# Two transformer layers on one core: feed forward's root on VectorE, layer 1's shifts by one product for two query blocks, new ranks and paces

## The chip, the cores and the metric

One core of a Trainium2 chip runs the whole program. Five engines work at the same time, each through its own queue: TensorE (PE; its weight loads are listed as PEld), VectorE (DVE), ScalarE (ACT), GpSimd (POOL) and SyncE (SP), which here only starts transfers. The metric is the device time of one execution in microseconds (us); less is better.

## The reference

Input x is 4 sequences (B) of 512 positions (T) by 128 channels (D), float32. There are 16 heads of 8 channels in both layers.

```python
xn = layernorm(x)                                   # layer 0
s = attention0(xn, ...)                             # below
g = silu(moe0(xn))
x = x + s * g
xn = layernorm(x)                                   # layer 1
s = block1(xn, ...)                                 # below
g = silu(moe1(xn))
x = x + s * g

# attention0: q, k with RMS norm per head, 4 value heads; mask: j <= i and j >= i - 64
a = (q @ k.T / sqrt(8)) * mask
denom = mean(sigmoid(a), axis=-1) + 0.5             # over all 512 keys
fitness = 1 / (denom * sum(1 / denom, over queries))
s = softmax(a * fitness[:, None] - 1e10 * (1 - mask)) @ v @ w_o + b_o

# moe0: 8 experts 128 -> 512 -> 128, GELU; a token goes to the larger index of its top two; times 2

# block1: layernorm, then windows of 64 positions that start 16 before every multiple of 32 ...
attn = softmax(q[window] @ k[window].T / sqrt(8)); wo = attn @ v[window]
# ... each window's first part is blended linearly with the one before; then
h = out @ wproj + bproj + xn
s = gelu(layernorm(h) @ w1 + b1) @ w2 + b2 + h      # feed forward, 128 -> 512 -> 128

# moe1: 8 experts 128 -> 512 -> 128, ReLU; a token goes to the expert of the largest logit
```

Layer 1's input is normed twice: once before the layer, once inside `block1`, whose residual is the first norm's result.

## The kernel before

All of x stays on the chip. The work is cut into threads, Python generators such as `scores_k1` or `feed1`. Most of them run over batches b = 0 to 3, and within one over four tiles of 128 positions, 16 tiles in all; the expert threads run over 23 blocks of up to 128 tokens of one expert.

**Order.** Which thread goes next is decided when the program is built, not by hand. `run` holds for every thread what its next step needs, takes the thread whose needs are there first in a modelled time, and among equal ones the one with the lowest rank for its batch (the four numbers behind each thread, L1485 on). `spent(cost, steps, events)` moves the modelled time on by `pace()` times TensorE's cost and places the step's work on VectorE ("D"), ScalarE ("A") and GpSimd ("G") in modelled queues; `copied` uses them to choose ScalarE or VectorE for a copy. TensorE works in the order in which the threads issue. On the other engines the order is fixed as the program is built, after the threads' order and the instructions' dependences. Where the model has a gap on TensorE, `awake` puts in products of `ones16` whose result is overwritten (warm-up products).

**Layer 0.** `prepare0` norms x and transposes it (`tr_xn`, `xnT`), `logits` gives the gate's `lg`, `route` works out which token goes into which block (`off`, `tok_blk`, `in_place`, and the product `tokens`). `moe_x` gathers blocks (`xb`, an indirect transfer by GpSimd, and its transpose `xt`), `moe_h` and `moe_y` do the two expert products (h, y) and put results back (`yt`, indirect too). `project0`, `scores_q` (s tiles, maxima `mx`, tanh `th`, sums `sm`), `fitness0`, `scores_k` (e tiles, exponentials `pt`), `values0` (`ov`), `outs0` and `combine0` are the attention.

**Layer 1.** `prepare1` norms (`xr`, `xn1`, transposed as `tr_xn1`) and gives the gate's logits; `project1` norms a second time and makes keys and queries `kd`, `qd`. `queries1` does a tile of 128 positions: the masked keys `k4` on VectorE, masked queries `q4` on GpSimd, values `v`, the s tile (scores with queries as rows, 32 products), and the maxima over keys `mx` (L1290). The maxima, negated, are the softmax's shift. The second score tile e, with keys as rows, needs that shift along its columns. So `split` (L465) writes each as three bf16 terms into `shb`, which is transposed (`tr_sh`), copied by ScalarE (`shd`, L1298) and multiplied by four masks (`sh4`, L1301; the trace calls it `sh`). `scores_k1` adds it: e is 32 products of kd and q4 and, on top, products of a matrix of ones with `sh4`:

```python
for w in range(2):
    for g in range(G):
        r = slice(32 * g, 32 * g + NS * J)
        mm(
            ps[g // 2][w * KB : (w + 1) * KB, g % 2, par], ones16[r, 0:KB],
            sh4[r, par, :, w * KB : (w + 1) * KB], start=False, stop=True,
        )
```

`w` is one of two query blocks of 64 (KB) in a tile, `par` one of the two overlapping sets of windows, `g` a group of four heads. `values1`, `outs1`, `contexts1` finish the attention. `feed1` (twice a batch, for two tiles each) does the product `pr`, the norm's moments `mv_d`, the root `rs_d`, `hn`, its transpose `tr_hn`, the two products f and fy. `combine1` writes the result. The experts run beside it, as in layer 0.

**The two roots.** `rsqrt` is an addition on VectorE (L392) and a power of -1/2 on GpSimd (L393). `rsqrt_many` (L395) does the root on VectorE by shifts and three Newton steps, 13 operations; layer 0's RMS norm uses it. `feed1` calls `rsqrt` (L1434).

Of the kernel before, what the change touches and what calls it, by code (L numbers as in the profile page):

```python
# [57 lines left out]
def two_layers(  # L58
# [22 lines left out]
    def mm(*args, **kw):  # L81

        ins = nc.tensor.matmul(*args, **kw)  # L83
        tc.stamp_issue_order_token(ins.ins, "pe")
        return ins
# [185 lines left out]
    def after(event):  # L271

        return None, max(0.0, at[event] - max(now["T"], now["-"]))
# [53 lines left out]
    def pace():  # L327
        return 1.8 if now["T"] < 70.0 else 1.12
# [66 lines left out]
    def rsqrt_many(dst, src, scale, eps):  # L395

        n = dst.shape[1]
        x = small.tile([P, n], F32, tag="rq_x", name=f"rq_x_{dst.tensor.name}", bufs=1)
        nc.vector.tensor_scalar(x, src, scale, eps, ALU.mult, ALU.add)
        y = small.tile([P, n], F32, tag="rq_y", name=f"rq_y_{dst.tensor.name}", bufs=1)  # L400
        nc.vector.tensor_single_scalar(y.bitcast(I32), x.bitcast(I32), 1, ALU.logical_shift_right)
        nc.vector.tensor_scalar(y.bitcast(I32), y.bitcast(I32), -1.0, float(0x5F3759DF), ALU.mult, ALU.add)
        nc.vector.tensor_scalar_mul(x, x, -0.5)
        z = small.tile([P, n], F32, tag="rq_z", name=f"rq_z_{dst.tensor.name}", bufs=1)
        for i in range(3):
            nc.vector.tensor_tensor(z, y, y, ALU.mult)
            nc.vector.tensor_tensor(z, z, x, ALU.mult)
            nc.vector.scalar_tensor_tensor(dst if i == 2 else y, z, 1.5, y, ALU.add, ALU.mult)
# [83 lines left out]
    def route(mask, n):  # L492
# [7 lines left out]
        with tc.high_priority():  # L500
# [53 lines left out]
            spent(0.35, [("D", 1.0)] * 7, [("rows", n)])  # L554
            in_places = []
            for q in range(2):
# [5 lines left out]
                spent(0, [after(("rows", n)), ("D", 1.2)], [("places", n, q)])  # L562
# [351 lines left out]
    shbs1 = prepared("shb1_", 2, [P, 2, G, 32], BF16)  # L914
    later.close()
# [288 lines left out]
    def project1():  # L1204

        for b in range(B):
            yield "-", [("xn1", b), ("s1", (b - 1) * NT - 1)]
# [30 lines left out]
    def queries1():  # L1238


        for i in range(NTILE):
# [52 lines left out]
            split(shb, mx, f"1_{b}_{t}")  # L1294
            spent(1.15, [("D", 2.45), ("D", 1.0)], [("s1", i), ("shb", i)], scores=1)
            yield "M", [("shb", i), ("e1", i - 2)]
            shd = att_p.tile([P, 2 * P], BF16, tag="shd1", name=f"shd1_{b}_{t}")
            nc.scalar.copy(shd, transposed16(shb.rearrange("p a g r -> p a (g r)"), 2, f"sh1_{b}_{t}"))  # L1298
            sh4 = att_p.tile([P, 2, J, P], BF16, tag="sh4_1", name=f"sh4_1_{b}_{t}")
            for j in range(J):  # L1300
                nc.vector.tensor_scalar_mul(sh4[:, :, j], shd.rearrange("p (a f) -> p a f", a=2), smask[:, j : j + 1])  # L1301
            asked1[i] = q4, sh4, v
            spent(0.13, [("A", 0.4), ("D", 1.2)], [("sh1", i)])

    def scores_k1():
        for i in range(NTILE):
# [9 lines left out]
            for par in range(2):  # L1316
# [8 lines left out]
                for w in range(2):  # L1325
                    for g in range(G):
                        r = slice(32 * g, 32 * g + NS * J)
                        mm(
                            ps[g // 2][w * KB : (w + 1) * KB, g % 2, par], ones16[r, 0:KB],
                            sh4[r, par, :, w * KB : (w + 1) * KB], start=False, stop=True,  # L1330
                        )
# [3 lines left out]
            spent(1.45, [("Ae", 1.03), ("Ae", 1.03)], [("e1", i)], scores=2)  # L1335
# [77 lines left out]
    def feed1():  # L1413


        for b in range(B):
            for u in range(0, NT, 2):
# [53 lines left out]
    def combine1():  # L1471
# [13 lines left out]
        (moe_h(0, gelu), 0, 59, 111, 16),  # L1485
        (scores_k1(), 87, 25, 32, 64),
        (project1(), 92, 81, 14, 102),
        (queries1(), 107, 26, 4, 78),
        (combine0(), 19, 20, 21, 22),
        (moe_load(0, xd0, w1_0, C_B1_0), 109, 42, 85, 68),  # L1490
        (moe_load_2(0, w2_0, b2_0), 18, 74, 23, 2),
        (gates(0, yt0), 56, 5, 6, 8),
        (values1(), 66, 112, 86, 55),
        (prepare0(), 31, 65, 95, 50),
        (moe_load(1, xd1, w1_1, C_B1_1), 35, 84, 34, 38),
        (moe_load_2(1, w2_1, b2_1), 101, 118, 37, 44),
        (scores_q(), 70, 36, 104, 94),
        (moe_x(0), 73, 93, 43, 96),
        (contexts1(), 11, 12, 54, 13),
        (project0(), 88, 106, 63, 62),  # L1500
        (moe_y(0, yt0), 117, 82, 90, 41),
        (moe_x(1), 67, 40, 46, 72),
        (gates(1, yt1), 103, 49, 114, 10),
        (values0(), 48, 15, 115, 124),
        (scores_k(), 33, 1, 58, 97),
        (route(mask0, 0), 45, 100, 24, 76),
        (fitness0(), 79, 61, 91, 69),
        (combine1(), 29, 30, 39, 99),
        (route(mask1, 1), 51, 83, 9, 75),
        (moe_y(1, yt1), 121, 71, 113, 127),  # L1510
        (outs0(), 47, 57, 125, 119),
        (masked0(), 7, 52, 53, 17),
        (moe_h(1, relu), 60, 3, 122, 105),
        (prepare1(), 27, 108, 28, 80),
        (outs1(), 120, 110, 116, 89),
        (feed1(), 126, 98, 123, 77),
# [45 lines left out]
```

## Time and profile before

| | |
|---|---|
| six runs: median, lowest, highest | 497.13, 491.62, 500.22 us |
| the profiled execution | 497.53 us |
| its span, first to last instruction | 495.8 us |
| mean granted TensorE clock | 0.911 |
| busy: PE, DVE, ACT, POOL | 419.7, 339.4, 261.8, 179.6 us |

The stations of the span, read from the order of time: layer 0's product `tokens` at 44.0, its first e tile at 86.2 and fifth at 121.2; its last expert product y ends at 175.2; layer 1's first transpose is at 196.4, its first s tile at 222.3, its first gathered block's transpose at 335.9, the first e tile of the last batch at 426.5 and the last at 458.9, and the last but one fy at 480.1.

How to read it: busy times of the engines overlap, so they do not add up to the span. A line of the order of time has the start (us from the span's start), the duration, the engine, the line of the code, the operation with output and inputs, shapes, and in brackets how long the engine idled before it and what ended that. A line of a group has the busy time and the mean ns of one, then the idle time before them and what ended most of it. A granted clock of 1.00 is TensorE's full speed.

### The profile page before, as it was taken

What the parts mean: (1) busy time and instruction counts of PE and PEld (TensorE: products, weight loads), DVE (VectorE), ACT (ScalarE), POOL (GpSimd) and SP (SyncE); (2) the same over time, 40 slices, a digit from 0 to 9 for tenths busy, and PEclk for the clock granted to TensorE, in tenths of its full rate; (3) what the DMA queues carried; (4) which work ended last, traced back from release to release, by engine and by line L of the source; (5) the groups of instructions that cost most, each with busy time, mean ns of one, the idle gap of its engine ahead of it and who ended that gap; (6) DMA issues with size and microseconds to landing.
All of it is one profiled execution on the core that took longest, in us unless ns stands there. A gap on an engine that the chain in (4) does not pass through costs nothing.

```text
span 495.8 us, 14720 instructions
## 1 busy us (share of the span) xinstructions
PE 419.7 (85%) x5663; PEld 297.5 (60%) x5663; DVE 339.4 (68%) x1013; ACT 261.8 (53%) x513; POOL 179.6 (36%) x251
## 2 busy tenths in 40 slices
PE   4978797999898658599999897798999993899985
PEld 2653475676565433365565564666879882688863
DVE  5699998562856988668773583984677770676465
ACT  1432574788577545564646654444676452345532
POOL 5760445455442222332410313136352336532311
PEclk8588599999999987679999997978999998799989
DMA  5404444757353011100000000050452782451131
GB/s 171 130 1 111 136 127 128 224 140 200 64 115 95 12 54 44 42 1 3 3 22 4 1 1 22 3 156 24 129 156 87 195 212 77 127 135 54 43 101 44
DMA packets 61894, 42.12 MB, mean 85 GB/s; under 512 B 11328, under 2 KB 54208, under 8 KB 61824
## 3 DMA queue, kind: packets, MB, share of 16 engines
q1 hardware_dynamic: 58464, 34.85, 25.4%
q0 software_dynamic: 2944, 6.04, 4.9%
q8 instruction: 45, 0.74, 0.6%
q10 hardware_dynamic: 416, 0.29, 0.3%
q14 instruction: 25, 0.20, 0.1%
HBM read 34.99 MB, written 6.16 MB: 83 GB/s over the span
## 4 chain that ended last, share of the span: by engine, by line
PE 50%; DVE 26%; issue 8%; ACT 8%; POOL 4%; DMA 3%; SPq 0%; DVEq 0%; POOLq 0%; ACTq 0%
PE e L83 9%; PE h L83 6%; PE s L83 6%; PE y L83 5%; PE ov L83 4%; DVE mx L1290 3%; DVE mx L1009 3%; PE fy L83 3%; PE f L83 3%; PE qkv L83 2%; PE o L88 2%; PE v L83 2%; ACT pt L1106 2%; ACT th L1017 1%; DVE sm L1009 1%
## 5 line engine op out<-in xcount | busy, mean ns | idle before, releaser
L666 POOL DMA_INDIRECT yt<-yb,put_at x46 | 46.3, 1006 | 100.8 <-DVE yb L664 15.5
L609 POOL DMA_INDIRECT xb<-xd,tokens_at x46 | 45.2, 983 | 52.6 <-DVE tokens_at L586 17.2
L83 PE MATMUL h<-xbT,wb 128*128 128x128 f32 x368 | 51.6, 293 | 2.2 <-ACT xbT L344 1.3
L83 PE MATMUL y<-wb,hb 128*128 128x128 f32 x368 | 49.1, 281 | 3.6 <-ACT hb L696 3.2
L83 PEld LDWEIGHTS h<-xbT,wb 128*128 128x128 f32 x368 | 46.9, 204 | 8.1 <-issue 3.3
L83 PEld LDWEIGHTS y<-wb,hb 128*128 128x128 f32 x368 | 45.3, 195 | 7.1 <-ACT hb L696 3.9
L83 PE MATMUL e<-q,kd 32*64 32x256 f32 (+1 forms) x864 | 44.4, 451 | 0.4 <-ACT pt L1106 0.4
L1333 ACT ACTIVATE pt<-e 128x1024 f32<-128x1024 f32 x32 | 31.0, 1022 | 20.7 <-PE e L83 20.6
L1290 DVE TENSOR_REDUCE mx<-s 128x16 f32<-128x1024 f32 x32 | 37.6, 1218 | 5.3 <-PE s L83 5.1
L1017 ACT ACTIVATE th<-s 128x768 f32<-128x768 f32 x32 | 26.0, 812 | 26.4 <-DVE mx L1009 25.8
L83 PE MATMUL s<-k,qd 32*32 32x384 f32 (+1 forms) x1024 | 37.7, 481 | 2.3 <-ACT pt L1333 2.0
L83 PEld LDWEIGHTS <-ones 12*64 12x64 bf16 (+2 forms) x439 | 21.6, 108 | 27.7 <-issue 19.3
L1106 ACT ACTIVATE pt<-e 128x1024 f32<-128x1024 f32 x32 | 31.0, 1021 | 13.3 <-PE e L83 13.2
L1009 DVE TENSOR_REDUCE mx<-s 128x8 f32<-128x768 f32 x32 | 29.3, 948 | 10.8 <-PE s L83 10.8
L344 ACT COPY osb<-ov 128x512 f32<-128x512 f32 x33 | 18.5, 587 | 28.5 <-PE ov L83 23.2
L696 ACT ACTIVATE hb<-h,bb 128x128 f32<-128x128 f32 x92 | 26.4, 381 | 10.4 <-PE h L83 9.9
L1009 DVE TENSOR_REDUCE sm<-th 128x8 f32<-128x768 f32 x32 | 30.0, 946 | 1.3 <-ACT th L1017 1.0
L83 PE MATMUL ov<-pt,va 64*32 64x128 f32 (+1 forms) x896 | 30.3, 302 | 0.4 <-DVE ctx L344 0.2
L83 PEld LDWEIGHTS e<-q,kd 32*64 32x64 f32 x864 | 19.3, 138 | 11.2 <-issue 5.8
L1251 POOL TENSOR_TENSOR q<-qd,jmask 128x640 f32<-128x640 f32 x16 | 19.9, 1258 | 15.3 <-PE e L83 13.9
L83 PE MATMUL e<-sh,ones 12*64 12x256 bf16 (+1 forms) x320 | 20.6, 309 | 3.6 <-DVE sh L1301 3.6
L704 ACT ACTIVATE hb<-h,bb 128x128 f32<-128x128 f32 x56 | 15.8, 375 | 14.2 <-PE h L83 11.6
(287 smaller groups left out, 907.0 us busy)
## 6 DMA issues: line engine op xcount, KB each, us to landing
wb<-in_w SPq DMA_DIRECT2D x92, 256.0 KB
bb<-in_b SPq DMA_DIRECT2D x46, 64.0 KB
acc<-yt SPq DMA_DIRECT2D x8, 256.0 KB
xd<-ln_a SPq DMA_DIRECT2D x4, 256.0 KB
xd<-xr SPq DMA_DIRECT2D x4, 256.0 KB
out<-acc SPq DMA_DIRECT2D x8, 128.0 KB
x<-in_x SPq DMA_DIRECT2D x3, 256.0 KB
bb<-in_cols SPq DMA_DIRECT2D x46, 2.0 KB
```

The source lines that it names most:

```text
L83: ins = nc.tensor.matmul(*args, **kw)
L344: (nc.scalar.copy if e == "A" else nc.vector.tensor_copy)(dst, src)
L609: nc.gpsimd.indirect_dma_start(out=xb, out_offset=None, in_=xd, in_offset=bass.IndirectOffsetOnAxis(ap=tokens_at[:, k : k + 1], axis=0),)
L666: nc.gpsimd.indirect_dma_start(out=yt, out_offset=bass.IndirectOffsetOnAxis(ap=routed[n][0][:, k : k + 1], axis=0), in_=y, in_offset=None,)
L696: nc.scalar.activation(h[:, c, :], src[:, c * P : (c + 1) * P], AF.Gelu, bias=bias[:, c : c + 1])
L704: nc.scalar.activation(dst, src_c, AF.Relu, bias=b)
L1009: nc.vector.tensor_reduce(dst[:, t, 8 * gg : 8 * gg + 8].rearrange("p (u j) -> p u j", u=2), src.rearrange("p u (j f) -> p u j f", j=J), A ...
L1017: nc.scalar.activation(th, ps[gg], AF.Tanh, scale=0.5 * SCALE)
L1106: nc.scalar.activation(pt[:, 2 * gg : 2 * gg + 2], ps[gg], AF.Exp)
L1251: engine.tensor_tensor(dst, src[:, None, o : o + TW].to_broadcast([P, J, TW]), jmask[:, :, None].to_broadcast([P, J, TW]), ALU.mult,)
L1290: nc.vector.tensor_reduce(mx.rearrange("p a g j -> p g a j")[:, 2 * gg : 2 * gg + 2], ps[gg], AX.X, ALU.max, negate=True,)
L1333: nc.scalar.activation(pt[:, 2 * gg : 2 * gg + 2], ps[gg], AF.Exp, scale=SCALE)
```

## The change

Three things, in one diff. (1) `feed1` calls `rsqrt_many`; its three work tiles are made 128 wide and cut to the width needed, since sizes now differ under one tag. (2) In layer 1 `split` writes into `terms`, and a product with `own` (which holds whether a position lies in block 0 or 1 of its tile) puts them into both halves of `shb`, so that a term stands in the half of its own block and the other half is zero. A product with `fold` (two identity matrices of 64 beside each other on the rows) takes the place of the transpose and puts both blocks into one set of 64 columns; `sh4` is half as wide; and one product of 32 rows with `lane` (ones where row and output block belong together) adds both blocks' shifts. `own`, `fold`, `smask1` and `lane` are made once, at the first step of `project1`. (3) `pace`, some costs and all ranks are different; the ranks come from a search in a model with the trace's paces.

```diff
@@ -325,7 +325,7 @@
             at[e] = t
 
     def pace():
-        return 1.8 if now["T"] < 70.0 else 1.12
+        return 1.45 if now["T"] < 70.0 else 1.08
 
     def behind_steps(e, t):
 
@@ -395,13 +395,13 @@
     def rsqrt_many(dst, src, scale, eps):
 
         n = dst.shape[1]
-        x = small.tile([P, n], F32, tag="rq_x", name=f"rq_x_{dst.tensor.name}", bufs=1)
+        x = small.tile([P, P], F32, tag="rq_x", name=f"rq_x_{dst.tensor.name}", bufs=1)[:, 0:n]
         nc.vector.tensor_scalar(x, src, scale, eps, ALU.mult, ALU.add)
-        y = small.tile([P, n], F32, tag="rq_y", name=f"rq_y_{dst.tensor.name}", bufs=1)
+        y = small.tile([P, P], F32, tag="rq_y", name=f"rq_y_{dst.tensor.name}", bufs=1)[:, 0:n]
         nc.vector.tensor_single_scalar(y.bitcast(I32), x.bitcast(I32), 1, ALU.logical_shift_right)
         nc.vector.tensor_scalar(y.bitcast(I32), y.bitcast(I32), -1.0, float(0x5F3759DF), ALU.mult, ALU.add)
         nc.vector.tensor_scalar_mul(x, x, -0.5)
-        z = small.tile([P, n], F32, tag="rq_z", name=f"rq_z_{dst.tensor.name}", bufs=1)
+        z = small.tile([P, P], F32, tag="rq_z", name=f"rq_z_{dst.tensor.name}", bufs=1)[:, 0:n]
         for i in range(3):
             nc.vector.tensor_tensor(z, y, y, ALU.mult)
             nc.vector.tensor_tensor(z, z, x, ALU.mult)
@@ -551,7 +551,7 @@
                 tok_blk[:, :, 0], in_blk, tile_at[:, :, None].to_broadcast([P, NTOK, NBLK]), ALU.mult
             )
             nc.vector.tensor_scalar_mul(tok_blk[:, :, 1], in_blk, pidx)
-            spent(0.35, [("D", 1.0)] * 7, [("rows", n)])
+            spent(0.35, [("D", 0.47)] * 7, [("rows", n)])
             in_places = []
             for q in range(2):
                 in_place = att_p.tile([P, NTOK // 2, P], BF16, tag="osb0", name=f"in_place_{n}_{q}")
@@ -559,7 +559,7 @@
                 for u in range(NTOK // 2):
                     nc.vector.tensor_single_scalar(in_place[:, u], place_at, placef[:, i + u : i + u + 1], ALU.is_equal)
                 in_places.append(in_place)
-                spent(0, [after(("rows", n)), ("D", 1.2)], [("places", n, q)])
+                spent(0, [after(("rows", n)), ("D", 0.65)], [("places", n, q)])
 
             past = of([1, NBLK, E], "past")
             nc.vector.tensor_tensor(
@@ -912,6 +912,11 @@
             ves[i][:, 0 : H * VC].rearrange("p (h d) -> p h d", d=VC)[:, :, HD], valid[:, i : i + 1].to_broadcast([P, H])
         )
     shbs1 = prepared("shb1_", 2, [P, 2, G, 32], BF16)
+
+    own = const.tile([P, 2], BF16, tag="own", name="own")
+    fold = const.tile([P, KB], BF16, tag="fold", name="fold")
+    lane = const.tile([P, P], BF16, tag="lane", name="lane")
+    smask1 = const.tile([P, J], F32, tag="smask1", name="smask1")
     later.close()
 
 
@@ -1204,6 +1209,18 @@
     def project1():
 
         for b in range(B):
+            if b == 0:
+                yield "-", [("mask", 0)]
+                half = small.tile([P, 2, 2], F32, tag="half", name="half", bufs=1)
+                nc.vector.tensor_reduce(half[:, 0], ident.rearrange("p (w q) -> p w q", w=2), AX.X, ALU.add)
+                nc.vector.tensor_copy(own, half[:, 0])
+                nc.vector.tensor_tensor(fold, ident16[:, 0:KB], ident16[:, KB:P], ALU.add)
+                nc.vector.tensor_reduce(
+                    smask1, ident.rearrange("p (g s j) -> p j g s", g=2 * G, j=J)[:, :, :, 0:NS], AX.XY, ALU.add
+                )
+                nc.vector.tensor_reduce(half[:, 1], ident.rearrange("p (g c r) -> p c g r", g=G, c=2), AX.XY, ALU.add)
+                nc.vector.tensor_copy(lane.rearrange("p (c k) -> p c k", c=2), half[:, 1, :, None].to_broadcast([P, 2, KB]))
+                spent(0, [("D", 1.3)], [("lane", 0)])
             yield "-", [("xn1", b), ("s1", (b - 1) * NT - 1)]
             xh = tok.tile([P, NT, D], F32, tag="ln", name=f"xh_{b}", bufs=3)
             with behind_steps("A", at["xn1", b]):
@@ -1291,16 +1308,26 @@
                     mx.rearrange("p a g j -> p g a j")[:, 2 * gg : 2 * gg + 2], ps[gg], AX.X, ALU.max, negate=True,
                 )
             shb = shbs1[i % 2]
-            split(shb, mx, f"1_{b}_{t}")
-            spent(1.15, [("D", 2.45), ("D", 1.0)], [("s1", i), ("shb", i)], scores=1)
+            terms = small.tile([P, 2, G, NS * J], BF16, tag="terms", name=f"terms_{b}_{t}", bufs=1)
+            split(terms, mx, f"1_{b}_{t}")
+            nc.vector.tensor_tensor(
+                shb.rearrange("p a g (c r) -> p (a g) c r", c=2)[:, :, :, 0 : NS * J],
+                terms.rearrange("p a g r -> p (a g) r")[:, :, None].to_broadcast([P, 2 * G, 2, NS * J]),
+                own[:, None, :, None].to_broadcast([P, 2 * G, 2, NS * J]), ALU.mult,
+            )
+            spent(1.15, [("D", 2.45), ("D", 1.25)], [("s1", i), ("shb", i)], scores=1)
             yield "M", [("shb", i), ("e1", i - 2)]
-            shd = att_p.tile([P, 2 * P], BF16, tag="shd1", name=f"shd1_{b}_{t}")
-            nc.scalar.copy(shd, transposed16(shb.rearrange("p a g r -> p a (g r)"), 2, f"sh1_{b}_{t}"))
-            sh4 = att_p.tile([P, 2, J, P], BF16, tag="sh4_1", name=f"sh4_1_{b}_{t}")
+            shd = att_p.tile([P, 2, KB], BF16, tag="shd1", name=f"shd1_{b}_{t}")
+            ps = bank(f"sh1_{b}_{t}")[:, 0 : 2 * KB].rearrange("p (a f) -> p a f", a=2)
+            for par in range(2):
+                mm(ps[:, par], shb[:, par].rearrange("p g r -> p (g r)"), fold, start=True, stop=True)
+            nc.scalar.copy(shd, ps)
+
+            sh4 = att_p.tile([P, 2, J, KB], BF16, tag="sh4_1", name=f"sh4_1_{b}_{t}")
             for j in range(J):
-                nc.vector.tensor_scalar_mul(sh4[:, :, j], shd.rearrange("p (a f) -> p a f", a=2), smask[:, j : j + 1])
+                nc.vector.tensor_scalar_mul(sh4[:, :, j], shd, smask1[:, j : j + 1])
             asked1[i] = q4, sh4, v
-            spent(0.13, [("A", 0.4), ("D", 1.2)], [("sh1", i)])
+            spent(0.1, [("A", 0.33), ("D", 0.9)], [("sh1", i)])
 
     def scores_k1():
         for i in range(NTILE):
@@ -1322,17 +1349,13 @@
                             ps[g // 2][w * KB : (w + 1) * KB, g % 2, par], kd[r, t * P + o : t * P + o + KB],
                             q4[r, :, o : o + KB], start=True, stop=False,
                         )
-                for w in range(2):
-                    for g in range(G):
-                        r = slice(32 * g, 32 * g + NS * J)
-                        mm(
-                            ps[g // 2][w * KB : (w + 1) * KB, g % 2, par], ones16[r, 0:KB],
-                            sh4[r, par, :, w * KB : (w + 1) * KB], start=False, stop=True,
-                        )
+                for g in range(G):
+                    r = slice(32 * g, 32 * g + 32)
+                    mm(ps[g // 2][:, g % 2, par], lane[r], sh4[r, par], start=False, stop=True)
             for gg in range(2):
                 nc.scalar.activation(pt[:, 2 * gg : 2 * gg + 2], ps[gg], AF.Exp, scale=SCALE)
             pts1[i] = pt, v
-            spent(1.45, [("Ae", 1.03), ("Ae", 1.03)], [("e1", i)], scores=2)
+            spent(1.25, [("Ae", 1.03), ("Ae", 1.03)], [("e1", i)], scores=2)
 
     def values1():
         for i in range(NTILE):
@@ -1431,9 +1454,9 @@
                 nc.vector.tensor_tensor(res[:, two], ps, res[:, two], ALU.add)
                 mv = moments(res[:, two], f"d{b}_{u}")
                 rs = small.tile([P, 2], F32, tag="rs", name=f"rs_d{b}_{u}")
-                rsqrt(rs, mv[:, :, 1], LN_EPS)
+                rsqrt_many(rs, mv[:, :, 1], 1.0, LN_EPS)
                 centred(hn[:, two], res[:, two], mv, rs)
-                spent(1.0, [("D", 0.7), ("D", 0.7), ("G", 1.0), ("D", 0.7)], [("pr", b, u)])
+                spent(1.0, [("D", 0.7), ("D", 0.75), ("D", 0.75), ("D", 0.75)], [("pr", b, u)])
                 nc.gpsimd.tensor_tensor(
                     res[:, two], res[:, two], row("ffn2")[:, None, :].to_broadcast([P, 2, D]), ALU.add
                 )
@@ -1482 +1505 @@
     run([
...
-        (scores_k1(), 87, 25, 32, 64),
-        (project1(), 92, 81, 14, 102),
-        (queries1(), 107, 26, 4, 78),
...
+        (scores_k1(), 2, 60, 111, 116),
+        (project1(), 120, 51, 106, 46),
+        (queries1(), 25, 29, 32, 3),
...
-        (moe_y(1, yt1), 121, 71, 113, 127),
...
-        (prepare1(), 27, 108, 28, 80),
-        (outs1(), 120, 110, 116, 89),
-        (feed1(), 126, 98, 123, 77),
+        (moe_y(1, yt1), 47, 23, 5, 19),
...
+        (prepare1(), 107, 0, 115, 22),
+        (outs1(), 95, 66, 100, 110),
+        (feed1(), 31, 59, 112, 69),
     ])
```

More of the change, by code (lines that the diff above doesn't have):

```diff
@@ L1484, in two_layers @@
     run([
-        (moe_h(0, gelu), 0, 59, 111, 16),
-        (scores_k1(), 87, 25, 32, 64),
-        (project1(), 92, 81, 14, 102),
-        (queries1(), 107, 26, 4, 78),
[L1489 to L1508, printed above, removed]
@@ L1509, in two_layers @@
-        (route(mask1, 1), 51, 83, 9, 75),
-        (moe_y(1, yt1), 121, 71, 113, 127),
-        (outs0(), 47, 57, 125, 119),
-        (masked0(), 7, 52, 53, 17),
-        (moe_h(1, relu), 60, 3, 122, 105),
-        (prepare1(), 27, 108, 28, 80),
-        (outs1(), 120, 110, 116, 89),
-        (feed1(), 126, 98, 123, 77),
+        (moe_h(0, gelu), 97, 58, 67, 24),
+        (scores_k1(), 2, 60, 111, 116),
+        (project1(), 120, 51, 106, 46),
+        (queries1(), 25, 29, 32, 3),
+        (combine0(), 89, 90, 92, 93),
@@ new lines, in two_layers @@
+        (moe_load(0, xd0, w1_0, C_B1_0), 77, 21, 39, 96),
+        (moe_load_2(0, w2_0, b2_0), 12, 7, 8, 9),
+        (gates(0, yt0), 70, 82, 83, 85),
+        (values1(), 105, 53, 126, 103),
+        (prepare0(), 91, 101, 109, 127),
+        (moe_load(1, xd1, w1_1, C_B1_1), 55, 44, 10, 73),
+        (moe_load_2(1, w2_1, b2_1), 80, 26, 117, 42),
+        (scores_q(), 13, 14, 15, 16),
+        (moe_x(0), 113, 41, 4, 78),
+        (contexts1(), 34, 36, 54, 37),
+        (project0(), 102, 94, 28, 81),
@@ new lines, in two_layers @@
+        (moe_y(0, yt0), 86, 48, 63, 98),
+        (moe_x(1), 79, 49, 76, 118),
+        (gates(1, yt1), 35, 74, 108, 119),
+        (values0(), 65, 52, 114, 68),
+        (scores_k(), 88, 45, 64, 87),
+        (route(mask0, 0), 6, 27, 30, 33),
+        (fitness0(), 40, 1, 43, 62),
+        (combine1(), 17, 18, 50, 72),
+        (route(mask1, 1), 57, 71, 75, 84),
+        (moe_y(1, yt1), 47, 23, 5, 19),
+        (outs0(), 121, 99, 20, 61),
+        (masked0(), 122, 123, 124, 125),
+        (moe_h(1, relu), 104, 56, 11, 38),
```

## The prediction

> **What bounds the kernel now.** I read the page's busy times first, then the chain that ended last, then a table by stretch, then each engine's order of time where the table shows a hole.
>
> ```profile
> PE 419.7 (85%) x5663; PEld 297.5 (60%) x5663; DVE 339.4 (68%) x1013; ACT 261.8 (53%) x513; POOL 179.6 (36%) x251
> ...
> PE 50%; DVE 26%; issue 8%; ACT 8%; POOL 4%; DMA 3%; SPq 0%; DVEq 0%; POOLq 0%; ACTq 0%
> ```
>
> TensorE (PE) is the engine with most work, but it carries only half of the chain; VectorE (DVE) carries a quarter. So the time is PE's 420 us plus 76 us in which PE waits for somebody. Where those lie (columns after the stretch: its length, then busy us and count of PE, PE's weight loads, VectorE, ScalarE, GpSimd, and the granted clock):
>
> ```profile
> 160.00:200.00 40.00, 25.76 (x302) 15.02 (x301) 35.53 (x93) 18.85 (x37) 10.20 (x11) 0.87 0.12 36
> 360.00:400.00 40.00, 38.83 (x692) 33.34 (x685) 28.23 (x79) 24.08 (x58) 15.73 (x16) 1.00 0.56 151
> 400.00:440.00 40.00, 29.35 (x472) 24.23 (x471) 19.66 (x58) 14.90 (x43) 21.20 (x21) 0.87 0.54 138
> 470.00:495.80 25.80, 19.04 (x106) 13.43 (x104) 14.66 (x44) 7.04 (x15) 3.40 (x4) 0.93 0.27 79
> ```
>
> PE is full at 360. It lacks 14 us at 160 to 200 (VectorE 35.5 of 40: the hand-over from layer 0 to 1), 11 us at 400 to 440, 7 us at the end. The hole at 400 is one stall:
>
> ```profile
> 408.67 0.16 DVE L392 TENSOR_SCALAR rs_d<-mv_d 128x2 f32<-128x2 f32 x1
> 409.19 0.76 DVE L1301 TENSOR_SCALAR sh<-shd,smask 128x256 bf16<-128x256 bf16 x3 [0.37 <-ACT shd L1298]
> 422.91 0.60 DVE L428 TENSOR_SCALAR hn<-xr,mv_d,rs_d 128x128 f32<-128x128 f32 x2 [12.96 <-POOL rs_d L393]
> ...
> 421.11 1.00 POOL L666 DMA_INDIRECT yt<-yb,put_at  x1 [0.30 <-issue]
> 422.14 0.73 POOL L393 TENSOR_TENSOR rs_d<-rs_d,neghalf 128x2 f32<-128x2 f32 x1
> ...
> 423.40 0.66 PE L88 MATMUL tr_hn<-ident,hn 128*128 128x128 f32 x2 [10.23 <-DVE hn L428]
> ...
> 424.76 1.71 PE y L83 x8
> 426.46 2.16 PE e L83 x48
> ```
>
> Feed forward's root is one GpSimd power (L393). It stands there behind GpSimd's gathers, puts and two `q4`; VectorE idles 12.96 us in front of `hn`, PE 10.23 us.
>
> **Part 1, the root by VectorE.** Removed, 8 times: the add (0.17) and the power (0.73). An undisturbed one takes 1.06 us from add to `hn` (484.16 to 485.22). Added: 13 VectorE operations on 128x2, each needing the one before. Such operations on 128x4 start 0.20 apart:
>
> ```profile
> 191.15 0.17 DVE L437 TENSOR_SCALAR w<-mv_b 128x4 f32<-128x4 f32 x1
> 191.35 0.18 DVE L438 RECIPROCAL w<-w 128x4 f32<-128x4 f32 x1
> ```
>
> 13 x 0.20 = 2.6, so 1.6 us longer each, 12.8 for eight. The last two roots stand alone in the tail, nothing hides them: 3.2. The other six (9.6) are covered while PE has products queued (PE 38.8 of 40 at 360); I take a third, 3.2. Sum **+6.4**, ends +3.2 and +12.8. Behind the root on VectorE stand `hn`, the maxima `mx` and the copies that free PSUM; PE waits for them.
> The big stall goes: 10.23, and the half clock behind it. The eight y products take 1.71 there against 0.89 at 409.25 and the e tile 2.16 against 1.39: 1.6. Sum **-11.8**, ends -11.8 and 0 (rival D). GpSimd also loses 8 x 0.73 from its queue, which I count at nothing: it is 36% busy. Next late is PE's own queue.
> [...]
>
> **Part 2, layer 1's shifts.** PE, per tile: 16 shift products of 12 rows x 64 columns become 8 of 32 x 128. An e tile takes 1.39 (434.00), the s tile with the same 32 products and no shifts 1.05 (410.14): the 16 cost 0.34. The nearest row for the new form is layer 0's, twice as long:
>
> ```profile
> L83 PE MATMUL e<-sh,ones 12*64 12x256 bf16 x256 | 13.8, 283 | 3.6 <-DVE sh L1301 3.6
> L83 PE MATMUL e<-sh,ones 12*128 12x512 bf16 x64 | 6.7, 412 | 0.0
> ```
>
> 6.7/64 = 105 ns, half of it 52, x 8 = 0.42: +0.08 a tile, **+1.3** for 16. Ends: half the old cost (-2.7), and four new ones as dear as four of layer 0 (0.84 a tile, +8). The two transposes become products half as wide: 32 x up to 0.06, **-1**, ends -2 and 0.
> [...]
> VectorE: `sh4` is 64 operations of 128x256 at 15.7/64 = 0.245; the new 128x128 ones are like `in_place`, 5.5/32 = 0.172: -4.7. The added product with `own`, 128x192, lies between `in_place` (0.17) and `tok_blk` (128x368, 0.53): 0.27 x 16 = +4.3. Net 0, under PE. But `own` stands between `split` and PE's product, whose predecessor waited 3.0 us in all for `shb`: **+0.7**, ends 0 and +4.3. ScalarE's copy gets shorter by 0.1, off the path. Part 2: +1.0.
> Six setup operations stand on VectorE before `off0`, for which ScalarE waits 5.96 us at the start: two reductions of 0.28, `smask1` 0.23, a copy 0.28, two of 0.15, less overlap: **+1.2**, ends 0 and +1.5.
>
> **Part 3, the order.** I counted in the built order what each engine has between two products, and priced it by the mean busy time of its groups.
> Hand-over: from layer 0's fifth e tile (121.2) to the last layer-0 expert product y (175.2), to layer 1's first transpose (196.4), to its first s tile (222.3), PE had 47.9, 14.0, 16.2 us of work and VectorE 38.5, 18.1, 20.0. It now has 34.0, 27.0, 14.6 and 27.9, 11.8, 34.1. So more PE work covers the layer's hand-over, and VectorE's part of its chain shrinks. These two holes should close:
>
> ```profile
> 186.91 0.61 PE L83 MATMUL e<-bands_k,diag 32*32 32x512 bf16 x2 [4.45 <-ACT th L1017]
> 203.20 1.87 PE L83 MATMUL lg<-gate_sb,xnT 128*128 128x8 f32 x8 [5.54 <-ACT xnT L344]
> ```
>
> That is 10 us, but VectorE's 34.1 against PE's 14.6 afterwards gives some back. I take half, **-5**, ends -10 and +10 (rival C).
> Tail: from the last e tile to the last but one fy PE had 17.8 us of work in 21.2; now 11.3, since an f and two y went ahead. That can save 6.5 or, if they only push others, nothing: **-4**.
> Layer 1's routing: between the token product and the first gathered block PE now has 3.4 us of filler, before 3.9 and an e tile, against a gather of 5.09: **+2.5**, ends 0 and +4.
> SP issues the same 690 instructions; the gathers' queue is not longer. The number of ScalarE table loads stays at 26.
>
> **The sum.** -11.8 + 6.4 + 1.0 + 1.2 - 5 - 4 + 2.5 = -9.7. The profiled execution took 497.53 (span 495.8 and 1.7 around it), 0.4 above the median of six, 497.13. 497.5 - 9.7 = **488**.
>
> **Rivals.**
> A, the order closes all these waits: hand-over -10, tail -6.5, routing 0, roots +3.2: 488 - 13.2 = 475. For it: 76 us of PE waiting are there to be taken. Against: VectorE gets 12.8 us more work.
> B, all eight roots on the path: +6.4, so 494, no change that shows. For it: VectorE carries 26% of the chain. Against: GpSimd's power also held VectorE, 0.8 us each at best.
> C, slower: VectorE becomes the bound at layer 1's opening. Before, its 20.0 us took 25.9 there, 1.3 times; at that ratio 34.1 take 44.2. With 40 and 27 for the two stages ahead that is 111 where before had 101: +10 in place of -5, **503**. It decides slower once the opening lasts longer than about 39 us. For it: 15 of those 34 us are maxima and sums that need PE's s tiles first. Against: the rest can run ahead, under PE's 27.
> D, the change doesn't do what it says: GpSimd's queue is as late as ever, and the 10 to 12 us show up as PE waiting for `q4` or puts: 498 to 500. For it: GpSimd is busiest just there (21.2 of 40). Against: only `rs_d` was waited for by VectorE in that hole.
>
> **How the numbers follow.** About 1% (5 us) is what a measurement tells from no change. Forecast (484 to 492) 0.38; A 0.20; B 0.12; D 0.08; C 0.22. Faster 0.58, same 0.20, slower 0.22. The range 472 to 504 leaves a tenth on each side: A's far end, and C with the dear end of the products. The forecast's own range is 484 to 492.
>
> **What would show it.** Right: no wait of VectorE over 3 us before `hn`; 13 small operations some 2.6 us from first to `hn` in the tail; PE idle at the hand-over under 5 us; an e tile of layer 1 at 1.35 to 1.55. Wrong: PE waiting for `mx` after layer 1's first transpose (C), for `q4` in the experts' stage (D), or e tiles near 1.9.

## The result and the profile after

The changed kernel is slower: 517.17 us (median of 20 runs, 507.79 to 524.11) against 494.85 (46 runs, 491.31 to 500.22). The ratio is 1.034, 95% interval 1.031 to 1.038, so about +17 us where 9.7 less were forecast. (The ratio leaves out the runs that fell in a slower state of the chip, so it is smaller than that of the medians.) The profiled execution took 512.12, its span 510.1.

The page, the waits of TensorE (us in total, times, longest), and four stretches with the columns used above:

```profile
PE 422.2 (83%) x5535; PEld 293.4 (58%) x5535; DVE 358.2 (70%) x1119; ACT 263.2 (52%) x525; POOL 176.9 (35%) x243
```

```profile
PE s L83 <- ACT th L1022: 13.3, 12, 3.4
PE tr_hn L88 <- DVE hn L428: 8.4, 5, 3.4
PE xt L88 <- DMA xb<-xd,tokens_at: 8.2, 5, 4.3
PE sh L83 <- DVE shb L1313: 8.1, 5, 2.5
```

```profile
160.00:200.00 40.00, 34.14 (x391) 18.77 (x390) 29.08 (x80) 24.14 (x39) 9.85 (x11) 0.91 0.11 34
360.00:400.00 40.00, 38.52 (x542) 31.78 (x541) 25.77 (x82) 22.26 (x62) 20.19 (x22) 1.00 0.53 148
400.00:440.00 40.00, 34.17 (x461) 27.92 (x460) 25.84 (x86) 17.72 (x45) 21.83 (x21) 0.96 0.59 162
470.00:510.10 40.10, 29.24 (x314) 21.81 (x312) 22.03 (x82) 18.41 (x31) 3.15 (x3) 0.91 0.20 57
```

TensorE's work is as before (422 against 420), its waiting grew from 76 to 88 us. The holes that the prediction named are smaller: 160 to 200 has 34.1 of 40 (25.8 before), 400 to 440 has 34.2 (29.4), and no wait is longer than 5 us but the one at the start. In their place stand 26 waits of 1 to 4 us, 18 of them ended by VectorE (before, 14 and 8). By stations: layer 1's first s tile comes at 221.3 (before 222.3), the first e tile of layer 1's second batch at 296.1 (292.4), the routing's first product `rk` at 335.6 (316.4), and the end at 510.1 (495.8). The loss is made inside layer 1's attention and feed forward, not at its opening. Of the 19 us at `rk`, some 9 are the new order's own and come back later (part 3 below).

### The profile page after: what moved, and what is told of

Its sections match the earlier page's. It is cut to its first block, busy times and chain, and to the rows that moved or that the text cites. A ratio compares the mean times of both kernels' runs of the same rounds, so it can differ in the third digit from the quotient of the medians.

```text
span 510.1 us, 14563 instructions
## 1 busy us (share of the span) xinstructions
PE 422.2 (83%) x5535; PEld 293.4 (58%) x5535; DVE 358.2 (70%) x1119; ACT 263.2 (52%) x525; POOL 176.9 (35%) x243
## 5 line engine op out<-in xcount | busy, mean ns | idle before, releaser
L609 POOL DMA_INDIRECT xb<-xd,tokens_at x46 | 46.4, 1008 | 46.6 <-DVE rq_y_rs_d L402 16.6
L83 PE MATMUL y<-wb,hb 128*128 128x128 f32 x368 | 51.0, 290 | 1.0 <-ACT osb L344 1.0
L83 PE MATMUL h<-xbT,wb 128*128 128x128 f32 x368 | 50.0, 286 | 0.2
L83 PEld LDWEIGHTS y<-wb,hb 128*128 128x128 f32 x368 | 47.6, 204 | 4.1 <-issue 1.5
L83 PE MATMUL s<-k,qd 32*32 32x384 f32 (+1 forms) x1024 | 36.5, 477 | 2.1 <-ACT th L1022 1.6
L696 ACT ACTIVATE hb<-h,bb 128x128 f32<-128x128 f32 x92 | 27.0, 382 | 11.0 <-PE h L83 5.7
L1074 POOL TENSOR_TENSOR q<-q2d,wmask 128x512 f32<-128x512 f32 x16 | 16.9, 1057 | 30.4 <-ACT q2d L344 15.3
L83 PEld LDWEIGHTS <-ones 128*128 128x128 bf16 (+1 forms) x183 | 13.8, 102 | 23.5 <-issue 13.6
L83 PEld LDWEIGHTS ov<-pt,va 64*32 64x32 f32 (+1 forms) x896 | 17.8, 113 | 14.3 <-DVE xr L1491 4.8
L664 DVE TENSOR_TENSOR yb<-y,bb 128x128 f32<-128x128 f32 x46 | 13.1, 285 | 16.9 <-PE y L83 16.6
```

The lines of the kernel that those rows point to most:

```text
L609: nc.gpsimd.indirect_dma_start(out=xb, out_offset=None, in_=xd, in_offset=bass.IndirectOffsetOnAxis(ap=tokens_at[:, k : k + 1], axis=0),)
L696: nc.scalar.activation(h[:, c, :], src[:, c * P : (c + 1) * P], AF.Gelu, bias=bias[:, c : c + 1])
L1074: nc.gpsimd.tensor_tensor(q4, q2s[b][:, None, f].to_broadcast([P, J, P]), wmask[:, :, None].to_broadcast([P, J, P]), ALU.mult)
```

## The experiments

To tell the steps from their order, the order was frozen: the planner's picks, its choices of ScalarE or VectorE and its warm-up products were written down from one kernel and replayed in another, whose steps differ.

```diff
-                if best is None or key < best[0]:
+                if n_ == _PICKS[at_pick[0]]:
```

TensorE's order is then the same; on the other engines only a few instructions beside the exchanged ones move. "Before" below is the kernel before, measured beside them on the same chip. It took about 495 us on some chips and 506 to 508 on others, so only ratios are compared across chips.

**Steps and order, two by two.** First the old order:

```diff
-                rsqrt(rs, mv[:, :, 1], LN_EPS)
+                rsqrt_many(rs, mv[:, :, 1], 1.0, LN_EPS)
```

> The threads go in exactly the order of the kernel before (its picks, its copies' engines and its warm-up products written down and replayed); only feed forward's root is on VectorE. Theory O (the new order costs the time; the two edits alone do not): the 10.2 us stall at 413 goes and 3 to 6 us of roots come back, so 486 to 492. Rival E (the edits cost it: serial VectorE work in front of TensorE, which after's trace shows as 8.4 us of waiting for hn against 2.0 without the big stall): 497 to 502. Rival G (GpSimd's queue is late anyway): 494 to 498, with PE waiting for q4 or gathers in the place of hn.

The second had the four changed places of the shifts alone, the third both, the fourth the reverse.

> The order of the kernel before, replayed; only layer 1's shifts are new (one product for two query blocks, fold, own, lane, and their six setup operations, picked right after layer 0's expert mask as in the changed kernel). Theory O: 495 to 499, the products +3, the waits for shb +1 to +3, the transposes -1. Rival E: 502 to 508, since the product with own stands in front of PE in each of 16 tiles (after: 8.1 us of waiting for shb against 3.0).

> The order of the kernel before, replayed; both edits. Theory O: the sum of the two single ones, 488 to 494. Rival E: 503 to 510, near the changed kernel. If the edits get in each other's way on VectorE, above the sum of the single ones by 3 us or more.

> The other way round: the order of the changed kernel, replayed (its setup step left out), with the old root and the old shifts. Theory O: 505 to 513, as slow as the changed kernel. Rival E: 490 to 497. In between, at about 500, both have a share.

Measured: 1.003 (0.998 to 1.008), 1.011 (1.005 to 1.017), 1.013 (1.007 to 1.020), 0.999 (0.995 to 1.004). Neither theory holds: the order alone costs nothing, and the edits alone do not make 1.034. So each edit was run alone in the new order.

> The order of the changed kernel, replayed; the root on VectorE, the shifts as before. In the old order the root alone changed nothing (1.003) and the new order with old steps changed nothing (0.999). Theory R (the root is what the new order does not bear, since it works feed forward in between batches of scores): 505 to 512. Rival S (the shifts are): 496 to 501. Rival V (VectorE has too little room for both; each alone is harmless): 497 to 502 here, and near 504 with the shifts alone.

> The order of the changed kernel, replayed; layer 1's new shifts, the root by GpSimd as before. Theory R: 500 to 504, the 1.1 per cent that the shifts cost in the old order. Rival S: 508 to 513. Rival V: 502 to 505, and the changed kernel's 512 only with both.

These gave 1.042 (1.036 to 1.048) and 1.022 (1.010 to 1.033), on a chip whose kernel before takes 508. All four were then run on one chip.

> The same kernel as old_steps_new_order, beside the next three on one chip, since the runs of the new order so far came from two chips whose kernel before takes 495 and 508. Theory V (order alone harmless, each edit dear in it): ratio 0.995 to 1.005. Rival C (the chip made root_new_order's 1.042): 1.01 to 1.02 if this chip is like the second.

> The new order with the root alone. Theory V: 1.02 to 1.04 whatever the chip, 10 to 20 us above the kernel with neither. Rival C: at most 1.015 above it on one chip.

> The new order with the shifts alone. Theory V: 1.015 to 1.03. Rival S2 (the shifts cost the same 1.1 per cent in any order): 1.010 to 1.012 above the kernel with neither.

> The changed kernel itself. 1.03 to 1.04 as before. If it stands below the sum of the two single ones, the edits share a cover that either takes away; if at the sum, they cost independently.

| order | old steps | root | shifts | both |
|---|---|---|---|---|
| before's | 1 | 1.003 | 1.011 | 1.013 |
| changed kernel's | 1.002 (0.997 to 1.006) | 1.038 (1.032 to 1.044) | 1.016 (1.010 to 1.022) | 1.042 (1.035 to 1.048) |

The first row is from the four runs above, the second from one chip. Rival C falls: the chip did not make the 1.042. The root is nearly free in the old order; in the new one it costs 18 us by itself and 13 beside the new shifts. The shifts cost 1.1 per cent in the old order and 1.4 in the new (2.2 on the chip of 508, with a wide interval). Together they cost 4.0 per cent where the sum is 5.0, a difference inside the intervals. TensorE's waits for `hn` in the new order without and with the root, first and second line:

```profile
PE tr_hn L88 <- DVE hn L428: 2.2, 2, 1.5
```

```profile
PE tr_hn L88 <- DVE hn L428: 8.2, 5, 3.4
```

In the new order the old root has no long stall: 2.2 us in all, where the old order's profile had 12.2, with 10.23 in one place. There is little there for VectorE's root to gain.

**Where the root's price lies.** The same two profiles by stretch: from the first root to `rk` (two roots), on to the last e tile (four roots), and to the end (two), first without the root on VectorE, then with it. The columns are those used above:

```profile
275.00:325.50 50.50, 42.85 (x801) 32.02 (x785) 35.17 (x106) 29.37 (x52) 10.18 (x13) 0.97 0.03 7
325.50:466.50 141.00, 125.04 (x1848) 103.21 (x1846) 84.22 (x278) 69.30 (x169) 63.30 (x68) 0.95 0.43 120
466.50:494.30 27.80, 20.84 (x231) 15.98 (x229) 15.77 (x49) 13.42 (x24) 4.41 (x4) 0.98 0.26 77
```

```profile
280.20:337.00 56.80, 45.52 (x804) 34.05 (x786) 38.79 (x130) 29.81 (x52) 8.86 (x11) 0.88 0.02 6
337.00:479.90 142.90, 126.52 (x1848) 104.16 (x1846) 93.43 (x326) 69.37 (x169) 60.27 (x64) 0.94 0.44 119
479.90:512.40 32.50, 22.55 (x231) 16.96 (x229) 19.47 (x73) 13.30 (x24) 2.20 (x2) 0.94 0.23 66
```

The first two roots cost 6.3 us, the next four 1.9, the last two 4.7. The pair with the new shifts, `new_order_shift` and `new_order_both`, gives 6.4, 1.8 and 6.4. Ahead of the first root the executions differ too, by 5.2 us in the first pair and by -4.4 in the second, which no root can make; what counts is that the two pairs agree behind it. In the first stretch TensorE does the same products with and without the root, but is busy 45.5 us in place of 42.9, at a granted clock of 0.88 in place of 0.97. So 2.7 of the 6.3 us are TensorE at a lower clock and 3.6 are more waiting: 1.2 for `hn`, 1.4 for `lg`, whose addition (L718) stands behind the root on VectorE, and 1.1 for `shb`. The last comes from GpSimd: without the power in its queue a `q4` runs earlier, and while it runs a small VectorE operation on the way to `shb` takes 1.22 us, where it takes 0.16 in `new_order_none` (`new_order_root`'s order of time):

```profile
300.03 1.25 POOL L1251 TENSOR_TENSOR q<-qd,jmask 128x640 f32<-128x640 f32 x1 [1.15 <-PE e L83]
300.10 1.22 DVE L471 CAST shb<-rest 128x32 bf16<-128x32 f32 x1
```

**The stall's gain.** Only batch 2's two roots moved to VectorE, in the old order:

```diff
+                (rsqrt_many(rs, mv[:, :, 1], 1.0, LN_EPS) if b == 2 else rsqrt(rs, mv[:, :, 1], LN_EPS))
```

> The order of the kernel before, replayed; the root on VectorE only in batch 2's two calls, where GpSimd's power held PE for 10.2 us at 413; the other six stay with GpSimd. Theory L (the gain of that place is real and given back at the other roots, in the tail above all): 487 to 491. Rival K (the gain goes into a lower granted clock and into the next waits whatever the other roots do): 493 to 497.

> The same kernel as root_batch2, which ran on a chip whose kernel before takes 508 us and where the profile of own_only, with GpSimd's root, shows no wait of TensorE at that place. Theory D2: if this chip's kernel before takes about 495, a gain of the stall less the price of two roots, 0.985 to 0.995; on a chip of 508, 0.996 to 1.002 again. Rival K (the gain goes into the clock and the next waits): 0.996 to 1.002 on any chip.

Both gave 0.998 (0.994 to 1.003 and 0.994 to 1.002), on chips whose kernel before takes 508 and 506. That is what the second expectation gave for such a chip under either theory, so it does not decide. The stall is not the same everywhere. It is 10.2 us in the profile of before and 8.6 in `shift_old_order`, on a chip of 495. In `own_only` below, also with GpSimd's root but on the first of these two chips, the transpose of `hn` follows `pr` after 12.5 us, 8.9 of them filled with work, against 16.2 and 5.8 in the profile of before. In `root_old_order`, on a chip of 495, the place was won: its `tr_hn` came 9.2 us earlier than before and the last e tile still 5.4, but the end only 0.9, since the stretch with the last two roots took 41.4 us in place of 36.9.

**The shifts' wait.** Everything as before, with one product more on VectorE between `split` and the transposes:

```diff
             split(shb, mx, f"1_{b}_{t}")
+            part = shb.rearrange("p a g r -> p (a g) r")[:, :, 0 : 2 * NS * J]
+            nc.vector.tensor_tensor(part, part, ones16[:, None, 0 : 2 * NS * J].to_broadcast([P, 2 * G, 2 * NS * J]), ALU.mult)
```

> The order of the kernel before, replayed; everything as before, but a product of shb with ones (128x192, in place) stands on VectorE between split and the transposes, as the product with own does in the changed kernel. It leaves the values as they are. Theory W (the shifts cost by this wait): 499 to 502, near the 502 of the new shifts. Rival P (they cost by PE's wider products): 495 to 497.

It gave 1.011 (1.007 to 1.015), all that the whole new shifts cost. The added product there, then the product with `own` in the changed kernel (line, operation, count, busy, mean ns):

```profile
L1296 DVE TENSOR_TENSOR shb<-shb,ones 128x192 bf16<-128x192 bf16 x16 | 5.0, 315 | 0.3
```

```profile
L1313 DVE TENSOR_TENSOR shb<-terms,own 128x192 bf16<-128x192 bf16 x16 | 5.6, 348 | 0.2
```

The added product is busy 5.0 us, and 1.1 per cent of 508 is 5.5: it is paid in full. TensorE waits 9.1 us for `shb` there, where before has 3.0.

**What the root's price is made of.** Four kernels: more warm-up products at TensorE's waits; feed forward's later steps picked later; a root of 10 operations (`for i in range(1 if n == 2 else 0, 3)`); and the 13 operations behind `hn`, where nothing reads their result, beside the old root:

```diff
                 centred(hn[:, two], res[:, two], mv, rs)
+                rsqrt_many(small.tile([P, 2], F32, tag="st", name=f"unused_{b}_{u}"), hn[:, u, 0:2], 0.0, 1.0)
```

> The changed kernel, its order replayed, with 62 more warm-up products (128x512 of ones16, 0.21 us each at full clock) at the eleven places of layer 1 where its trace shows TensorE waiting 0.9 to 2.5 us for VectorE, so many that they fit into the wait. Theory C (a short wait costs more than itself: after a stretch of 3.4 us in which TensorE is busy under about 0.6, the next is granted half the clock, and the changed kernel has about twice as many such stretches in layer 1): 1.015 to 1.030 of the kernel before, against 1.034 to 1.042 for the changed kernel. Rival D (VectorE is the bound there, TensorE's clock follows): 1.033 to 1.045.

> The changed kernel, its order replayed, but with the four steps of feed forward that follow its first product (transpose, f, f, fy) picked two TensorE steps later in batches 0 and 1, where the new order leaves 2.9 to 4.4 us of TensorE work between that product and the transpose of hn, and hn takes 5.2. Theory T (the new order leaves too little work over the longer root): 1.015 to 1.030. Rival D: 1.033 to 1.045.

> The changed kernel, its order replayed, with two Newton steps in feed forward's root, 10 operations in place of 13 (its output differs in the last digits only). Theory T: some 0.6 us less in front of hn, eight times, and with it a quarter of the root's 18 us: 1.022 to 1.033. Rival D: as theory T if it is VectorE's load, since that falls too; the next kernel tells the two apart. No dose: 1.034 to 1.042.

> The new order with the old root by GpSimd and the old shifts (ratio 1.002), and the 13 operations of the new root put behind hn, into a tile that nobody reads. VectorE carries the root's load, but hn does not wait for it. Theory T (the length of the chain in front of hn costs): 1.002 to 1.015. Rival D (VectorE's load costs): 1.025 to 1.040.

Measured, beside a kernel before of 507: 1.037 (1.030 to 1.044), 1.058 (1.053 to 1.064), 1.039 (1.032 to 1.045), 1.052 (1.047 to 1.057). No changed kernel ran on that chip, so the first three are held against its 1.034 and 1.042 on others. The warm-up products won nothing, though TensorE's waits for `hn` fell from 8.4 to 5.5 and those for `shb` from 8.1 to 2.3. That speaks for rival D, but does not clear the clock: from the first s tile to `rk` they did not raise it (0.90 granted, 0.91 in the changed kernel), and the stretches above show it carrying a part. More work in front of `tr_hn` made it worse, though `hn` was then waited for only in the tail. And the 13 operations cost 5.0 per cent over the order alone, more than the root's 3.6, where `hn` does not need them. So theory T, that only the chain in front of `hn` is too long for the new order, fell; VectorE's time costs. By the price below, the 24 operations less of `two_newton` would be 0.7 per cent, inside the interval, so it tells nothing. No kernel put the same operations where VectorE has nothing waiting behind them, so its load and the place in its queue are not told apart.

Last, the same 13 operations in the old order:

> The order of the kernel before, replayed, with its own root by GpSimd and old shifts, and the 13 operations behind hn into a tile that nobody reads. Theory D2 (VectorE's time is paid nearly in full in either order, and in the old one the root's price was hidden in the sum because it closed the stall at 413): 1.015 to 1.025. Rival O2 (only the new order has no room on VectorE; in the old one the operations are covered): 0.998 to 1.008.

1.031 (1.026 to 1.035), above the range of either theory: 15.4 us of 506, on average 1.9 for each of the eight. `root_batch2_again` ran on the same chip in the same order; against it the three stretches grew by 5.5, 10.4 and 5.6 us (two of its middle four roots are on VectorE already). So in the old order the four in the middle were not covered. In the order of time, at one of them, the 13 operations stand directly ahead of the maxima, and these ahead of `shb`:

```profile
378.04 0.16 DVE L407 TENSOR_TENSOR rq_z_unused<-rq_z_unused,rq_x_unused 128x2 f32<-128x2 f32 x1
378.23 0.16 DVE L408 SCALAR_TENSOR_TENSOR unused<-rq_z_unused,rq_y_unused 128x2 f32<-128x2 f32 x1
378.31 2.35 DVE L1290 TENSOR_REDUCE mx<-s 128x16 f32<-128x1024 f32 x2
...
381.99 0.19 DVE L472 TENSOR_TENSOR shb<-rest,shb 128x32 bf16<-128x32 f32 x1
```

TensorE's waits, first with the 13 operations, then in `root_batch2_again`:

```profile
PE tr_sh L88 <- DVE shb L472: 9.0, 7, 3.4
...
PE e L83 <- DVE sh L1301: 6.9, 1, 6.9
```

```profile
PE e L83 <- DVE sh L1301: 3.6, 1, 3.6
PE tr_sh L88 <- DVE shb L472: 3.3, 5, 1.7
```

Nothing waits for the 13 results; the waits of TensorE grow at the next tile's shifts. That is one way in which a root's time reaches TensorE at places that do not name it.

## Why the prediction was wrong

**The root's length was right, its cover was not.** The tail after shows the chain alone:

```profile
495.44 0.17 DVE L399 TENSOR_SCALAR rq_x_rs_d<-mv_d 128x2 f32<-128x2 f32 x1
495.64 0.17 DVE L401 TENSOR_SCALAR rq_y_rs_d<-rq_x_rs_d 128x2 int32<-128x2 int32 x1
...
497.62 0.16 DVE L408 SCALAR_TENSOR_TENSOR rs_d<-rq_z_rs_d,rq_y_rs_d 128x2 f32<-128x2 f32 x1
497.81 0.60 DVE L428 TENSOR_SCALAR hn<-xr,mv_d,rs_d 128x128 f32<-128x128 f32 x2
```

2.37 us from the first to `hn`, predicted 2.6; not all 13 need the one before, as the prediction had it (L403 starts 0.07 after L402). The step that failed is "I take a third, 3.2" for the six roots ahead of the tail, with the cover "PE has products queued (PE 38.8 of 40 at 360)". In the new order that cover was there for the four roots in the experts' stage, which cost 1.9 us together, less than a third of their 6.4 (1.6 each, as predicted). It was not there for the two ahead of the routing. They cost 6.3, over twice their own lengthening of 1.3 each (2.37 in place of 1.06): as shown above, TensorE waits for the root, for what stands behind it and for a `q4` that moved, and then works at a lower clock. That GpSimd's freed time counts for nothing, as the prediction had it, was wrong there. The last two, taken at 3.2, cost 4.7 to 6.4. And in the old order, from whose profile the 38.8 of 40 was read, the middle four were not covered either: a busy TensorE says nothing on what its next products wait for. Behind the root on VectorE stand `mx`, `shb` and `sh4` of the next tile; I named such instructions ("`hn`, the maxima `mx` and the copies") and then priced them at a third. Measured without the old root's stall in the sum, the root's price is 13 us (new order, beside the new shifts), 15.4 (old order, operations behind `hn`) and 18 (new order, by itself), at or above my upper end of 12.8.

**The stall was counted as a gain of the root in an order that did not have it.** This is the largest miss in the sum. "Sum -11.8" came from the old order's profile, and part 3 then counted the new order's gains on top. The new order by itself leaves 2.2 us of waits for `hn` and gives the rest back elsewhere. For the old order's null, `root_old_order` shows a part of the account: 9.2 us won at the stall, 4.5 lost again at the last two roots. That a price of some 15, less the stall and the power's own waits, makes up the whole of it was put together from different kernels and chips, not shown in one.

**Part 2: the wait was mis-sized, and so were the products.** `own` was taken at 0.7 of "ends 0 and +4.3"; it costs 5.5. The transposes came as predicted. The products did not: an e tile before, then after,

```profile
433.93 0.69 PE L83 MATMUL e<-q,kd 32*64 32x256 f32 x16
434.41 0.32 PE L83 MATMUL e<-sh,ones 12*64 12x256 bf16 x8
434.52 0.75 PE L83 MATMUL e<-q,kd 32*64 32x256 f32 x16
434.96 0.43 PE L83 MATMUL e<-sh,ones 12*64 12x256 bf16 x8
435.32 0.71 PE L83 MATMUL v<-wqkv_sb,xhT 128*128 128x128 f32 x4
```

```profile
456.51 0.69 PE L83 MATMUL e<-q,kd 32*64 32x256 f32 x16
457.13 0.29 PE L83 MATMUL e<-sh,lane 32*128 32x256 bf16 x4
457.35 0.69 PE L83 MATMUL e<-q,kd 32*64 32x256 f32 x16
457.97 0.29 PE L83 MATMUL e<-sh,lane 32*128 32x256 bf16 x4
458.19 0.23 PE L83 MATMUL sh<-fold,shb 128*128 128x64 bf16 x2
```

1.39 became 1.68: +0.29 a tile, 4.6 in 16, where +0.08 was taken. The four new products are as dear as predicted (0.22, 55 ns each). But each sixteen ahead of them now hold TensorE 0.62, in place of 0.48 and 0.44, before the next form starts. Half of layer 0's product was not the nearest row for that; a change of form was in its row once (32x64 to 12x128, at 88.03 in the profile of before), here it comes four times a tile. Why TensorE is held 0.14 to 0.18 longer was not shown: no run changes the form alone. Since `own_only` alone costs as much as the whole of the shifts, these 4.6 us seem to lie under VectorE's wait, or to be made good by the shorter `sh4`; neither was tried by itself.

The six setup operations were taken at 1.2. The first wait for `ln_a` was 5.85 us after and 5.06 before, but it is 3.7 to 5.5 in the kernels without them and 4.5 to 6.0 in those with them, so little is to be read from it.

**Part 3 gave nothing.** -5, -4 and +2.5 were predicted; the order alone is 0.999 and 1.002. The single waits did move as forecast: those of `lg` for `xnT` are 1.3 us in all in place of 6.9, none of them at the hand-over. So did two of the stretches. In `new_order_none`, which has the order alone, layer 1's first s tile comes 3.5 us earlier than before, and the stretch from the last e tile to the end takes 27.8 in place of 36.9. But from the first s tile to `rk` it takes 106.7 in place of 94.1, with TensorE busy 6.6 us longer in it, and that stretch stood nowhere in the sum. A stretch with more work for TensorE is not a shorter program when another one takes up what it gives.

**The tail.** "3.2" for two roots: at the last one the wait costs twice.

```profile
498.22 0.58 PE L88 MATMUL tr_hn<-ident,hn 128*128 128x128 f32 x2 [2.07 <-DVE hn L428]
498.64 0.59 PE L83 MATMUL f<-ones 128*128 128x512 bf16 x2
499.46 3.64 PE L83 MATMUL f<-hT,fw_sb 128*128 128x256 f32 x8 [0.23 <-ACT hT L1469]
```

```profile
496.50:500.00 3.50, 1.56 (x5) 0.90 (x6) 3.22 (x12) 1.08 (x2) 1.10 (x1) 0.92 0.00 0
500.00:503.50 3.50, 3.50 (x11) 2.47 (x10) 2.25 (x6) 1.20 (x3) 0.00 (x0) 0.60 0.34 98
```

TensorE was busy 1.56 of 3.5 us, and the next 3.5 were granted 0.60. The eight f products took 3.64; before, at a granted 1.00, 1.99. So the last root's 1.3 became about 3. In the stretch ahead of the lower clock TensorE was not idle, but less than half of it was filled.

**The rivals.** C had the side and the engine right, VectorE, and the place wrong: its opening was to last longer than 39 us and took 22.4. B named the roots "all on the path" but at 6.4 in sum with the stall's gain in it. D did not come.

## What to carry to other kernels

An engine at 68% can have no room at all (VectorE, with 13 operations more at each root in the old order: 1.031): its instructions stand in a fixed order, and what counts is what stands behind the added ones and who waits for that. Price each addition at its own place: the same root cost 0.5 us in one stretch of the new order and 3.2 in another, with a length that grew by 1.3. Where a chain that TensorE waits for stands behind it, take the full length, and more if the new wait lowers TensorE's clock (here 0.88 granted in place of 0.97 in one stretch, 0.60 behind the last root); take as cover only what a trace shows to be idle on that engine just there. Do not add a stall's gain, read from the old order, to a new order's gains: a planner that moves everything has often moved the stall too. To judge an edit that comes with a new order, freeze the order and exchange the steps, both ways.

## What the runs showed of the hardware

In the tail's root of the changed kernel a VectorE operation on 128x2 starts 0.19 to 0.21 us after the one whose result it needs, and one that does not need the operation before it starts 0.07 after that; thirteen take 2.37. In two profiles a VectorE operation on 128x32 took 1.22 (`new_order_root`, 300.10) and 1.20 us (the changed kernel, 297.94) beside a GpSimd product on 128x640, and ended with it; a like one just ahead of the second took 0.16. Sixteen products of 32x64 held TensorE 0.62 us in the e tile after, where products of 32x128 follow, and 0.44 to 0.48 in the e tile before, where products of 12x64 follow.

TensorE's clock changes in these traces in pieces of 3.41 us. Counted over the twenty profiles, a piece at full clock in which TensorE was busy under 0.4 of the time was followed by half clock in 124 of 124 cases, one at 0.4 to 0.6 in 89 of 160, and one above 0.6 in 27 of 2096; under theory C's 0.6 it is 213 of 284. Half clock ended only behind a piece that was busy 0.8 or more (260 of 357, and 0 of 177 below that). In the profiles of before and after alone the five counts are 15 of 15, 8 of 18, 1 of 207, 24 of 36 and 0 of 15.

The same program took 495 us on some chips and 506 to 508 on others. In the old order with GpSimd's root, TensorE's longest wait for `hn` was 10.2 us in the profile of before and 8.6 in `shift_old_order`, on chips of 495; in `own_only`, on a chip of 508, its two waits for `hn` were 2.0 together. These three kernels differ in other steps.
